# Two layers over a graph on one core: where b_w's row, a weight in squares and the order of the last products stand

## Chip, core and metric

The kernel runs on one core of a Trainium2 chip. The metric is the device time of one execution in microseconds; less is better. A program counts its engines as PE (TensorE, matrix products; PEld is its loading of weights), DVE (VectorE), ACT (ScalarE), POOL (GpSimd) and SP (SyncE, which here only issues transfers). A core has 16 DMA engines, which all queues share.

## What is computed

x is 4096 x 512, adj is a 4096 x 4096 matrix of zeros and ones (int32, 1 in 128 set).

```python
# layer 0
keep   = (adj > 0) & (cumsum(adj > 0, axis=1) <= 64)
cnt    = keep.sum(axis=1)
xj     = leaky_relu((keep @ x / max(cnt, 1)) @ W_nb.T + b_nb)
xi     = leaky_relu(x @ W_line.T + b_line)
x1     = layernorm(x + xi + where(cnt > 0, xj, 0))
# layer 1
Wh     = x1 @ W + b_w
e      = leaky_relu_0.2((Wh @ a1 + b1)[:, None] + (Wh @ a2 + b2)[None, :])
e      = where(adj > 0, e, -9e15)
out    = layernorm(x1 + softmax(e, axis=1) @ Wh)
```

## The kernel before

Rows are worked in 32 blocks of 128. The order of every engine's instructions is that of the program text; nothing reorders them, so what stands ahead in a queue and waits holds up all behind it. Transfers issued from SP and ACT use eight completion semaphores in turn, here called lanes: each transfer first waits until the one eight places before it has landed.

**The maps of layer 0.** `x @ W_nb.T` and `x @ W_line.T` are taken first, block by block (`linear`, L337 to L344). The products need the weights and x turned. Two ways of turning occur. `turn_by_pe` (L279): VectorE copies a chunk of 128 rows with its columns reordered, four products with the identity turn it into PSUM, ACT copies it out. W_nb, W_line (`turn_w`, L328) and block 0 of x go this way. The other is by squares: the transfer puts 32-row bands of the source side by side on 32 partitions each (`load_turned_x`, L265), so that VectorE's transpose of 32 x 32 squares (L294) gives the whole turned tile. Blocks 1 to 31 of x go this way, loaded by POOL.

Behind the weights, SP loads W of layer 1 and the rows a1, a2 and b_w (`load_rows`, L346 to L350). `fold_w` (L352 to L361) multiplies them on VectorE to W @ a1 and W @ a2, and SP writes the result out (L361). The loads of adj (`load_adj`, L160) come next in SP's queue. Each adj chunk of 128 x 2048 goes through ACT (`edge`, L167), the running count on VectorE (`scan`, L179, and L184), and is packed and stored as one byte per entry. VectorE's order within a block of the maps is: turn the block after next, add the bias, add x, then the scans that are due (`codes_until`).

**The sums of layer 0.** For each block, 64 products of 128 x 512 (L509) add up the neighbours' rows, from the turned codes (`make_kt`, L249) and the mapped rows, kept in two parts, y_hi and y_lo. `finish` (L463) does the rest of a block in four parts during the next block's products: scale, add the own row (stored by the maps, loaded by SP, L504), normalise, dot with the folded rows. The scans go on through most of this stage.

**Layer 1's start.** W is loaded (L542), then b_w's row (L546), then x1 as squares (`load_turned`, L561, four transfers for one of 32 steps s), the own row of the last block (L777), and the first codes `nat` (`load_nat`, L608). `turn_x1` (L575) turns the squares of step s; the first three steps' turned tiles lie in `early`, which takes memory of layer 0. For each s, four products give Wh (L809), `finish_wh` (L584) adds b_w's row, and later steps carry the first two blocks' masks and scores and `combine_wh` (L597 to L600), which forms sums of quarters of Wh. At s = 22 and s = 26 `turn` (L685) and `combine` (L698 to L701) prepare the first two parts of the weights.

**Layer 1's sums.** Attention times Wh is done for 256 rows at a time (16 groups g), each in four parts k (q = 4g + k), by a scheme with seven products of half-size matrices instead of eight (`consume`, L710 to L728, on Wh's sums in `bt`). The seven results of a group lie in four PSUM banks, two to a bank and the seventh alone, as `where` (L708) says: (1,2), (4,7), (5,6), 3. The order of the products is that of `order` (L719), another one for the last part of all. The last group's results are put together and written out by the lines from L871 on.

```python
    top, low = (rows.tile([P, 2, HC], F32, name="c") for _ in range(2))
    nc.scalar.copy(top[:, 0], p[1])                 # L876
    tt(top[:, 1], top[:, 0], p[6], ALU.add)         # L877
    tt(top[:, 0], top[:, 0], p[2], ALU.add)         # L878
    tt(low[:, 0], top[:, 1], p[7], ALU.add)         # L879
```

Of the kernel before, what the change touches and what calls it, by code (L numbers as in the profile page):

```python
# [9 lines left out]
F32 = mybir.dt.float32  # L10
# [3 lines left out]
I32 = mybir.dt.int32  # L14
# [6 lines left out]
P = 128  # L21
SQ = 32
# [10 lines left out]
def two_layer_adj_gnn(  # L33
# [16 lines left out]
    nc = tc.nc  # L50
# [86 lines left out]
    with ExitStack() as l0:  # L137
# [117 lines left out]
        with ExitStack() as la:  # L255
# [44 lines left out]
            def early(name):  # L300
                dt = I32 if name == "a" else BF16
                t = adj_p.tile([P, CH], dt, name=name).bitcast(F32)
                return t.rearrange("p (c q) -> p c q", q=C)

            raw = {}
            for name in ("nb", "line"):
                t = early("a")
                raw[name] = [t[:, c, :] for c in range(NC)]
            raw["w"] = []
            for k in range(2):  # L310
                t = early("left")
# [6 lines left out]
            def load_w(name, src, queues):  # L318
                for c in range(NC):
                    queues[c % len(queues)].dma_start(raw[name][c], src[ts(c, P), :])  # L320
# [7 lines left out]
            def turn_w(name, idle=0):  # L328

                wt = wp.tile([P, NC, C], F32, name=f"wt_{name}")  # L330
                for c in range(NC):
                    if idle:
                        spin(idle)
                    turn_by_pe(wt[:, :, ts(c, P)], raw[name][c])
                w_t[name] = wt

            def linear(lhs_t, name):  # L337
                pl = ps_acc.tile([P, C], F32, name="acc")
# [42 lines left out]
            load_own_x(0, nc.sync)  # L381
            load_w("nb", w_nb, (nc.scalar, nc.sync))
            load_turned_x(1)
            load_w("line", w_line, (nc.sync,))
            nc.sync.dma_start(bias_line, b_line.partition_broadcast(P))
            load_w("w", w, (nc.sync,))
            load_rows(nc.sync)
# [5 lines left out]
            for i in range(NB):  # L393
                if i > 1:
                    load_own_x(i - 1, nc.gpsimd)
                if i > 0:
                    load_turned_x(i + 4)
                    turn_x(i + 2)
                xt = xts.pop(i)
                pys[i] = linear(xt, "nb")  # L400
                if i == 0:
                    turn_w("line")
                pls[i] = linear(xt, "line")
                if i == 0:
                    turn_x(1)
                    turn_x(2)
                    load_turned_x(4)
                nc.scalar.copy(y_hi[:, i, :], pys[i])
                if i > 0:
                    line(i - 1)  # L410
                if i > 1:
                    own(i - 2)
                if i == 0:
                    fold_w()
                if i > 0:
                    codes_until(min(i * AHEAD // (NB - 4), AHEAD))
                if i == NB - 3:

                    spare = adj_p.tile([P, CH], I32, name="a")
                    ktbs[0] = spare[:, : CH // 2].bitcast(BF16).rearrange(  # L420
                        "p (t i) -> p t i", t=NT
                    )
                    nc.sync.dma_start_transpose(ktbs[0], code_d[0])
                if i == NB - 1:
                    spare = adj_p.tile([P, CH], BF16, name="edge")
                    kts[0] = spare.bitcast(F32R).rearrange(
                        "p (t r i) -> p t r i", r=2, i=P
                    )
                    make_kt(0)
                nc.vector.tensor_tensor(  # L430
                    y_lo[:, i, :], pys.pop(i), y_hi[:, i, :].bitcast(F32), ALU.subtract
                )
                if i > 0:
                    bend(i - 1)
                if i == NB - 2:
                    load_late()
# [106 lines left out]
            ws[ts(n, SQ), :, :], w[ts(n, P), :].rearrange("(m b) c -> b m c", b=SQ)  # L543
        )
    bias_w = ep.tile([P, C], F32, name="res", bufs=1)
    nc.sync.dma_start(bias_w, b_w.partition_broadcast(P))  # L546


    bt = big.tile([P, NS // 2, 7, HC], F32, name="bt")
# [6 lines left out]
    def load_turned(s):  # L556

        if s < NS:
            part = x1_d[s // 8].rearrange("(n s a) c -> s a n c", s=8, a=SQ)[s % 8]
            for n in range(NC):  # L560
                nc.sync.dma_start(  # L561
                    x1s[ts(n, SQ), s % 4, :].rearrange("a (j c) -> a j c", c=P),
                    part[:, :, ts(n, P)],
                )
# [37 lines left out]
    def load_nat(b, h):  # L602

        if b < NB:
            nats[b, h] = ep.tile([P, 2, NS * SQ // 2], BF16, name="nat")
            rows = code_d[b].rearrange("(i a) (n x) -> n a i x", a=SQ, n=4)
            for n in range(4):
                nc.sync.dma_start(nats[b, h][ts(n, SQ)], rows[n][:, ts(h, 2), :])  # L608
# [96 lines left out]
        }  # L705


    where = {1: (0, 0), 2: (0, 1), 4: (1, 0), 7: (1, 1), 5: (2, 0), 6: (2, 1), 3: (3, 0)}  # L708

    def consume(q):  # L710
        g, k = divmod(q, NP)
        if k == 0:
            two = [ps_s.tile([P, 2, HC], F32, name="pt")]
            two += [ps_acc.tile([P, 2, HC], F32, name="acc") for _ in range(3)]
            banks[g] = {n: two[i][:, j, :] for n, (i, j) in where.items()}
        part = parts.pop(q)


        order = (1, 2, 4, 7, 5, 6, 3) if q < NP * NT - 1 else (4, 1, 2, 6, 7, 5, 3)  # L719
        for n in order:  # L720
            lhs, rhs = part[n]
            mate = [m for m in order if where[m][0] == where[n][0]]
            for j in range(4):
                nc.tensor.matmul(  # L724
                    banks[g][n], lhs[:, j, :], bt[:, 4 * k + j, rhs, :],
                    start=(k == 0 and j == 0 and n == mate[0]),
                    stop=(k == NP - 1 and j == 3 and n == mate[-1]),
                )  # L728
# [46 lines left out]
    for s in range(4):  # L775
        load_turned(s)
    nc.sync.dma_start(owns[NB - 1], own_d[NB - 1])  # L777
    load_nat(0, 0)
    load_nat(0, 1)
    for s in range(3):  # L780
        turn_x1(s)
        load_turned(s + 4)
    for g in range(4):
        finish(NB - 1, g)

# [19 lines left out]
    for s in range(NS):  # L805
        pws[s] = ps_acc.tile([P, C], F32, name="acc")
        x1t = x1ts.pop(s)
        for m in range(NC):
            nc.tensor.matmul(  # L809
                pws[s], x1t[:, m, :], ws[:, m, :], start=(m == 0), stop=(m == NC - 1)  # L810
            )
        if s > 0:
            finish_wh(s - 1)
        turn_x1(s + 3)
        load_turned(s + 7)
        if FIRST <= s < FIRST + 8:
            b, i = divmod(s - FIRST, NI)
            mask(b, i)
            score(b, i)
        if FIRST + 4 <= s < FIRST + 12:  # L820
            b, i = divmod(s - FIRST - 4, NI)
            if i == 0:
                greatest(b)
                shift(b)
            weigh(b, i)
        if s in (FIRST + 14, FIRST + 18):
            q = (s - FIRST - 14) // 4
            turn(q)
            combine(q)
        elif s >= FIRST + 8:  # L830
            combine_wh()
    finish_wh(NS - 1)
# [98 lines left out]
```

## Time and profile before

| | |
|---|---|
| median of 3 runs | 1612.21 us (1611.77 to 1615.34) |
| the profiled execution's own time | 1611.63 us |
| its span, first to last instruction | 1609.9 us |
| PE busy | 1583.8 us (98%) |
| DVE busy | 1328.1 us (82%) |
| ACT busy | 903.2 us (56%) |
| mean granted PE clock | 0.996 |
| maps of layer 0 | to about 236 us |
| sums of layer 0 | to about 704 us |
| Wh | about 710 to 826 us |
| sums of layer 1 | to about 1600 us |

Busy time is an instruction's time on its engine; products are pipelined, so a busy PE isn't PE at its peak. The granted clock is the share of full speed that PE was allowed. The chain of waits is followed back from the last instruction, at each step to what released it. Rows of a timeline give the start, the duration, the engine (SPq is SP's queue), the line, the operation and the tiles; in brackets stand the idle time before it and what ended it.

### The profile page before, as it was taken

What the parts mean: (1) busy time and instruction counts of PE and PEld (TensorE: products, weight loads), DVE (VectorE), ACT (ScalarE), POOL (GpSimd) and SP (SyncE); (2) the same over time, 40 slices, a digit from 0 to 9 for tenths busy, and PEclk for the clock granted to TensorE, in tenths of its full rate; (3) what the DMA queues carried; (4) which work ended last, traced back from release to release, by engine and by line L of the source; (5) the groups of instructions that cost most, each with busy time, mean ns of one, the idle gap of its engine ahead of it and who ended that gap; (6) DMA issues with size and microseconds to landing.
All of it is one profiled execution on the core that took longest, in us unless ns stands there. A gap on an engine that the chain in (4) does not pass through costs nothing.

```text
span 1609.9 us, 18503 instructions
## 1 busy us (share of the span) xinstructions
PE 1583.8 (98%) x6456; PEld 1221.9 (76%) x6456; DVE 1328.1 (82%) x2186; ACT 903.2 (56%) x1054; POOL 258.1 (16%) x396
## 2 busy tenths in 40 slices
PE   9999999999999999989999999999999999999997
PEld 5444448888888787854468888888888888888886
DVE  4999987999999999845798788888788888788863
ACT  2655556677676766413437655567655567655520
POOL 4455532222122222101000000000000000000000
PEclk9999999999999999999999999999999999999999
DMA  8887868767776676335211111111111111111100
GB/s 199 286 264 232 262 211 239 216 202 212 220 208 198 209 213 193 100 103 118 79 40 27 53 40 53 44 29 46 53 41 53 43 30 47 53 40 53 40 7 33
DMA packets 168365, 192.74 MB, mean 120 GB/s; under 512 B 101408, under 2 KB 134464, under 8 KB 160080
## 3 DMA queue, kind: packets, MB, share of 16 engines
q1 hardware_dynamic: 147968, 131.38, 29.6%
q0 software_dynamic: 19728, 59.27, 10.8%
q8 instruction: 50, 0.82, 0.2%
q10 hardware_dynamic: 576, 0.92, 0.2%
q14 instruction: 43, 0.35, 0.1%
HBM read 132.65 MB, written 42.08 MB: 109 GB/s over the span
## 4 chain that ended last, share of the span: by engine, by line
PE 69%; DVE 23%; DMA 3%; issue 2%; ACT 1%; POOL 1%; SPq 0%; DVEq 0%; POOLq 0%; ACTq 0%
PE acc L724 34%; PE pt L724 14%; DVE left L179 10%; PE acc L340 9%; PE acc L509 9%; PE acc L809 3%; DVE left L184 2%; DVE junk L487 2%; DVE own L475 1%; DVE st L117 1%; DVE t L471 1%; DMA a<-in_adj_dram 1%; DVE t L468 1%; DVE own L131 1%; DVE c L575 1%
## 5 line engine op out<-in xcount | busy, mean ns | idle before, releaser
L509 PE MATMUL acc<-y_hi,kt 128*128 128x512 f32 x1016 | 396.3, 390 | 2.9 <-ACT kt L249 2.9
L509 PE MATMUL acc<-y_lo,kt 128*128 128x512 f32 x1016 | 395.8, 390 | 0.0
L724 PE MATMUL acc<-bt,s 128*128 128x256 f32 x1536 | 342.1, 379 | 0.0
L724 PEld LDWEIGHTS acc<-bt,s 128*128 128x128 f32 x1536 | 292.3, 190 | 39.2
L621 ACT ACTIVATE w<-nat,few 128x1024 f32<-128x1024 uint8 x128 | 136.9, 1135 | 277.1 <-DVE a L685 237.0
L126 POOL TENSOR_TENSOR rs<-ve,few 128x1 f32<-128x1 f32 x64 | 76.1, 1190 | 1021.1 <-DVE ve L124 1021.1
L724 PE MATMUL acc<-bt,a 128*128 128x256 f32 x1024 | 231.6, 379 | 0.0
L724 PE MATMUL pt<-bt,a 128*128 128x256 f32 x1024 | 231.5, 379 | 0.0
L509 PEld LDWEIGHTS acc<-y_hi,kt 128*128 128x128 f32 x1016 | 190.7, 188 | 44.5 <-ACT kt L249 5.0
L509 PEld LDWEIGHTS acc<-y_lo,kt 128*128 128x128 f32 x1016 | 190.9, 188 | 39.3
L724 PEld LDWEIGHTS pt<-bt,a 128*128 128x128 f32 x1024 | 194.9, 190 | 26.5 <-issue 0.5
L724 PEld LDWEIGHTS acc<-bt,a 128*128 128x128 f32 x1024 | 194.9, 190 | 26.1
L685 DVE STREAM_TRANSPOSE a<-w 128x1024 f32<-128x1024 f32 x128 | 153.0, 1225 | 56.1 <-ACT w L666 53.2
L249 ACT ACTIVATE kt<-ktb,few 128x1024 fp32r<-128x1024 uint8 x124 | 139.8, 1148 | 84.7 <-PE acc L509 69.0
L167 ACT ACTIVATE edge<-a,few 128x2048 bf16<-128x2048 int32 x64 | 127.9, 1998 | 99.4 <-DVE left L184 78.0
L613 ACT ACTIVATE w<-w,st_n 128x1024 f32<-128x1024 f32 x128 | 149.4, 1234 | 49.8 <-DVE m L624 49.8
L624 DVE CUSTOM_DVE_ANT_0 w<-e_n,w 128x1024 f32<-128x1024 f32 x128 | 149.5, 1221 | 9.1 <-ACT w L621 7.7
L666 ACT ACTIVATE w<-w,nm 128x1024 f32<-128x1024 f32 x128 | 145.4, 1137 | 11.3 <-DVE nm L657 11.3
L179 DVE TENSOR_TENSOR_SCAN left<-few,edge 128x2048 bf16<-128x2048 f32 x32 | 141.3, 4416 | 12.3 <-ACT edge L167 11.2
L179 DVE TENSOR_TENSOR_SCAN left<-few,ends,edge 128x2048 bf16<-128x2048 f32 x32 | 143.2, 4476 | 0.0
L202 ACT CAST code<-left 128x2048 uint8<-128x2048 bf16 x64 | 120.6, 1884 | 7.6 <-DVE left L184 7.6
L340 PE MATMUL acc<-wt_nb,xt 128*128 128x512 f32 x256 | 115.4, 594 | 1.8 <-DVE xt L294 1.0
(135 smaller groups left out, 1528.5 us busy)
## 6 DMA issues: line engine op xcount, KB each, us to landing
a<-in_adj_dram SPq DMA_DIRECT2D x64, 1024.0 KB, 5.7
code_d<-code POOLq DMA_DIRECT2D x64, 256.0 KB, 5.2
nat<-code_d SPq DMA_DIRECT2D x256, 64.0 KB, 2.0
own_d<-xb POOLq DMA_DIRECT2D x32, 256.0 KB, 5.7
w<-x_d SPq DMA_DIRECT2D x128, 64.0 KB, 2.0
c<-in_x_dram POOLq DMA_DIRECT2D x124, 64.0 KB, 5.5
xb<-in_x_dram POOLq DMA_DIRECT2D x31, 256.0 KB, 5.7
own<-own_d SPq DMA_DIRECT2D x31, 256.0 KB, 2.7
```

The costliest lines, as they stand in the source:

```text
L167: nc.scalar.activation(edge_of[s], loaded.pop(s), AF.Sigmoid, bias=steep[:, 0:1], scale=STEEP, accum_out=cnts[:, h, b : b + 1],)
L179: nc.vector.tensor_tensor_scan(left, two.to_broadcast([P, CH]), e, NEIGHBORS + 2.0 if h == 0 else end, ALU.max, ALU.subtract,)
L202: nc.scalar.copy(code.bitcast(U8), seen_of.pop(s))
L249: nc.scalar.activation(kts[s], bytes_.rearrange("p t (i r) -> p t r i", r=2), AF.Sigmoid, bias=steep[:, 1:2], scale=STEEP,)
L340: nc.tensor.matmul(pl, lhs_t[:, k, :], w_t[name][:, k, :], start=(k == 0), stop=(k == NC - 1),)
L509: nc.tensor.matmul(accs[i], kt[:, k // 2, k % 2, :], term[:, j, :], start=(j == 0 and term is y_hi), stop=(j == NB - 1 and term is y_lo),)
L613: nc.scalar.activation(dst, src, AF.Prelu, bias=bias, scale=scale, alpha=0.2)
L621: nc.scalar.activation(w_i, nats[b, i // 2].bitcast(U8)[:, i % 2, :], AF.Relu, bias=far, scale=-FAR)
L624: nc.vector.tensor_tensor_reduce(w_i, e2_n, w_i, 1.0, -3e38, ALU.subtract, ALU.max, m4s[b][:, i : i + 1])
L666: nc.scalar.activation(w_i, w_i, AF.Exp, bias=nms[b][:, i : i + 1], accum_out=z4s[g][:, r, i : i + 1])
L685: nc.vector.transpose(a[:, r].rearrange("p s (i a) -> p i s a", a=SQ), wts[2 * g + r][:, :, ts(k, 8 * SQ)].rearrange("p i (s x) -> p i s x ...
L724: nc.tensor.matmul(banks[g][n], lhs[:, j, :], bt[:, 4 * k + j, rhs, :], start=(k == 0 and j == 0 and n == mate[0]), stop=(k == NP - 1 and ...
```

## The change

Five edits. W_line is loaded as squares of 32 and turned by four VectorE transposes (`turn_line`). The load of b_w's row moves behind the first seven steps of x1's squares, and the first loads of `nat` move into step s = 0. The last group of layer 1 gets its own order of products in all four parts, and the pairs in its banks follow that order: (4,1), (2,6), (7,5), 3. The first two parts' `turn` and `combine` are put at s = 22, 24, 26 and 28, one each.

```diff
-            for name in ("nb", "line"):
-                t = early("a")
-                raw[name] = [t[:, c, :] for c in range(NC)]
+            t = early("a")
+            raw["nb"] = [t[:, c, :] for c in range(NC)]
+
+            line_w = adj_p.tile([P, CH], I32, name="a").bitcast(F32)
+            line_w = line_w.rearrange("p (j c) -> p j c", c=P)
...
+            def turn_line():
+                wt = wp.tile([P, NC, C], F32, name="wt_line")
+                for c in range(NC):
+                    nc.vector.transpose(
+                        wt[:, :, ts(c, P)].rearrange("p m (j a) -> p j m a", a=SQ),
+                        line_w[:, ts(c, NC), :].rearrange("p j (m b) -> p j m b", b=SQ),
+                    )
+                w_t["line"] = wt
...
-            load_w("line", w_line, (nc.sync,))
+            for n in range(NC):
+                nc.sync.dma_start(
+                    line_w[ts(n, SQ)], w_line[:, ts(n, P)].rearrange("(j a) c -> a j c", a=SQ)
+                )
...
-                    turn_w("line")
+                    turn_line()
...
     bias_w = ep.tile([P, C], F32, name="res", bufs=1)
-    nc.sync.dma_start(bias_w, b_w.partition_broadcast(P))
...
-    where = {1: (0, 0), 2: (0, 1), 4: (1, 0), 7: (1, 1), 5: (2, 0), 6: (2, 1), 3: (3, 0)}
+    order = {True: (1, 2, 4, 7, 5, 6, 3), False: (4, 1, 2, 6, 7, 5, 3)}
+    where = {key: {n: divmod(i, 2) for i, n in enumerate(o)} for key, o in order.items()}
...
-            banks[g] = {n: two[i][:, j, :] for n, (i, j) in where.items()}
+            banks[g] = {n: two[i][:, j, :] for n, (i, j) in where[g < NT - 1].items()}
...
-        order = (1, 2, 4, 7, 5, 6, 3) if q < NP * NT - 1 else (4, 1, 2, 6, 7, 5, 3)
-        for n in order:
+        key = g < NT - 1
+        for n in order[key]:
             lhs, rhs = part[n]
-            mate = [m for m in order if where[m][0] == where[n][0]]
+            mate = [m for m in order[key] if where[key][m][0] == where[key][n][0]]
...
-    load_nat(0, 0)
-    load_nat(0, 1)
     for s in range(3):
         turn_x1(s)
         load_turned(s + 4)
+    nc.sync.dma_start(bias_w, b_w.partition_broadcast(P))
...
         load_turned(s + 7)
+        if s == 0:
+            load_nat(0, 0)
+            load_nat(0, 1)
...
-        if s in (FIRST + 14, FIRST + 18):
-            q = (s - FIRST - 14) // 4
-            turn(q)
-            combine(q)
+        if s in range(FIRST + 14, FIRST + 22, 2):
+            q, part = divmod((s - FIRST - 14) // 2, 2)
+            (turn, combine)[part](q)
         elif s >= FIRST + 8:
             combine_wh()
```

## The prediction, made before the changed kernel had run

> **What bounds the kernel now.** I read the page first (PE busy 98% of the span), then the chain of waits, because a busy share doesn't say which wait ends last, and then the timeline and the windows of the three places that the diff touches: the start, the boundary between the layers, the end. From about 714 us on, TensorE (PE) is the bound but for waits of 0.3, 2.2 and 0.7 us near 778, 782 and 818. Between 41 and 84 us and between 292 and 613 us the chain runs over VectorE (DVE), on the scans L179.
>
> The boundary, in SP's timeline (start, duration, what was issued):
>
> ```profile
> 679.99 1.85 SPq L542 DMA_DIRECT2D w<-in_L_gnn_W_dram  x4
> 704.02 0.35 SPq L546 DMA_DIRECT2D res<-in_L_gnn_bW_dram  x1
> 704.41 7.56 SPq L561 DMA_DIRECT2D w<-x_d  x16
> 712.06 0.38 SPq L777 DMA_DIRECT2D w<-own_d  x1
> ```
>
> SP stands still for 22 us in front of L546, the load of b_w's row: its buffer is layer 0's memory, released by the last products of L509. x1's squares (L561) queue behind it though their own buffers are free. The chain of waits in order of time shows what that costs:
>
> ```profile
> 613.22 91.01 PE acc L509 x400
> 704.23 0.14 SPq L546
> ...
> 705.83 2.97 DMA w<-x_d
> ...
> 708.92 0.72 DVE w L575
> ...
> 709.69 10.45 PE acc L809 x17
> ```
>
> PE ends layer 0 at 704.2 and starts layer 1 at 709.69. The windows (last columns: granted PE clock, DMA share, GB/s) show a second price:
>
> ```profile
> 704.00:707.00 3.00, 0.21 (x1) 0.00 (x0) 0.00 (x0) 0.00 (x0) 0.00 (x0) 1.00 0.37 120
> 709.60:712.00 2.40, 2.31 (x3) 1.17 (x4) 1.04 (x3) 0.00 (x0) 0.00 (x0) 0.50 0.53 138
> 712.00:714.00 2.00, 2.00 (x3) 0.67 (x2) 1.74 (x3) 0.00 (x0) 0.00 (x0) 0.50 0.52 162
> 716.00:718.00 2.00, 2.00 (x6) 0.93 (x5) 1.51 (x4) 0.00 (x0) 0.23 (x1) 1.00 0.49 148
> ```
>
> After the gap PE runs at half clock until about 715.5: the first 24 matmuls of L809 take 709.69 to 722.98 = 13.3 us, where 24 at the later pace of 0.429 us take 10.3.
>
> The start, in the same chain:
>
> ```profile
> 9.70 8.40 DMA edge<-in_L_gnn_a_dram
> ...
> 24.07 0.39 SPq L361
> ...
> 24.50 14.51 DMA a<-in_adj_dram
> ...
> 41.16 4.44 DVE left L179
> ```
>
> What sets the pace is not PE. a1's row lands at 18.1, `fold_w` (L356) runs, its result is written (L361), the first adjacency load follows in the same queue, and the first scan starts at 41.16. PE takes xt(5) at 48.4 and xt(6) at 56.5, each made right behind a scan.
>
> The end (start, duration):
>
> ```profile
> 1596.15 3.62 PE L724 MATMUL acc<-bt,s 128*128 128x256 f32 x16
> 1598.14 0.42 DVE L877 TENSOR_TENSOR c<-c,acc 128x256 f32<-128x256 f32 x1 [19.49 <-PE acc L724]
> ...
> 1598.93 0.41 DVE L879 TENSOR_TENSOR c<-c,acc 128x256 f32<-128x256 f32 x1
> ```
>
> L877 reads product 6, complete at about 1594.4, but 6 shares a bank with 5, which ends at 1597.9.
>
> [...] 5.5 us of idleness gave 0.50, while the waits of 1.8 us near 611 and 2.2 us near 782 left it at 1.00. [...] a reader waits for its neighbour in the bank, as L877 does. [...]
>
> **The change, part by part.**
>
> 1. b_w's row behind x1's squares. In the built order the first 16 loads of squares now wait for DMA lanes only, so they issue right after L542, from 681.9 (16 x 0.47 = 7.5 us), and land before 695. The wait for layer 0's last products passes to the load of own row 31 (L777) and to `turn_x1(0)`, whose target lies in layer 0's memory too. Queued behind L777 on SP: squares 4 to 6, then b_w, then squares 7. At 704.05 DVE starts `turn_x1(0)`, 0.71 us; PE starts at 704.05 + 0.71 + 0.06 = 704.8 instead of 709.69: **-4.9 us**. The gap becomes 0.6 us, far below those that left the clock alone: **-3.0 us**. What could be late next: own row 31 is issued at 704.1 and lands 3.6 us later (its delay before), 707.7. DVE's `finish(31)` comes behind three transposes, so L475 starts at about 708.2 (before: 715.73), and `turn_x1(3)` moves from 721.01 to 713.5, done 714.2; PE wants it at 704.8 + 3 x 3.43 = 715.1. Slack 0.9 us. b_w: after 0.4 us of own row and 12 squares x 0.45 from 704.85, issued at about 710.4, landing 3.6 us later at 714.0; `finish_wh(0)` wants it at 714.2. Tight, but PE is five blocks of PSUM away from needing that result.
>
> 2. The 8 loads of nat (1.8 us per 4) move on SP behind squares 7, to about 716 to 720. Squares 8 stand behind them, issued by 722.3, landed by 724.5; their transpose must wait for PE to end s = 5 at 725.4 anyway. ACT wants nat at s = 8, past 732. 0 us.
>
> 3. turn and combine apart (s = 22, 24, 26, 28). DVE has no idle time from 781 to 830, and the burst of 5.0 us at s = 26 (812.7 to 817.7) made `turn_x1(30)` late: PE's weight load at 819.09 shows 0.96 us idle against a usual 0.24. Now only 2.3 us stand there, and the transpose ends some 4 us sooner relative to PE: **-0.7 us**. Two `combine_wh` (1.65 us each) move to q = 0; PE wants their rows at q = 3, some 36 us later. The 0.3 and 2.2 us near 780 come from s = 12 to 19 and stay.
>
> 4. The last group's pairs (4,1), (2,6), (7,5), 3. L877 can start at 1594.7. L879 waits for the bank of 7 and 5, ended 1597.9, so it starts at 1598.14 instead of 1598.93, and all behind it on DVE moves with it: **-0.8 us**. PE does the same number of products in all groups.
>
> 5. The line weight by squares. Off PE: 16 products; off DVE four copies of 0.43; off ACT four copies. On DVE: four transposes of 0.70 = 2.8 us. Each reads all 128 partitions, so all four loads must have landed: before, the fourth had at 12.7 (it frees the lane of L348's third load). Then 12.9 to 15.7, and PE, done with the first map at 14.5, starts the second at 15.8 instead of 17.46. That 1.7 us is **lost**: xt(5) and xt(6) come from DVE behind scans, PE only waits longer for them (about 2 and 1.5 us, short enough for the clock). What counts is when a1 lands. The queues are saturated from 4 to 18 us (DMA share 1.05), so it is what the pieces cost. Rows: 868 packets took 51.8% of 16 engines for 10 us, 95 ns each. Squares of 512 B: at 798 to 816, 24.6% of 16 x 18 us over some 2,410 of them, 29 ns. Per engine 32 x 95 = 3.0 us becomes 128 x 29 = 3.8: **+0.7 us** (estimate), on the chain. Bounds: -0.3[...]; above, from 6 to 12 us, where POOL's squares mix in, the rate fell from 402 to 270 GB/s, which charges some 0.5 MB of squares with about 3.2 us, or +4 us for 1 MB. I take the packet price.
>
> Sum: -4.9 - 3.0 - 0.7 - 0.8 + 0.7 = **-8.7 us**. The profiled execution took 1611.63 us (span 1609.9), 0.6 below the runs' median 1612.21; taken off the median: **1603.5 us**.
>
> **The rivals.**
> - The clock stays halved behind the shorter gap, or the start of layer 1 finds another late input (own row, b_w): 3 us back, 1606.5. Against: 2.2 us gaps didn't do it, and the slack worked out above. 8%.
> - The start costs the upper bound: a1 lands 4 us late[...]: 1606.8 to 1610. For: saturated queues. Against: the packet price. 10%.
> - The change doesn't do what it says: `turn_x1(0)` still waits for something that comes after 704 by a load. Then only parts 3 to 5 count: -0.8, 1611.4. Against: the built order. 3%.
> - Slower: a piece costs by number, not by bytes. L361 writes 1,024 pieces of 4 B and lands after 11.3 us: 64 per engine, 177 ns each. At that price the line squares need 128 x 177 = 22.6 us, 19.6 more; a1 and all behind it are late by that, and 9.4 gained elsewhere leaves 1622. It turns to slower by over 0.2% at about 125 ns a piece. Against: squares of the same 512 B landed in 2.0 us (L561). 3%.
> - The forecast: 76%.
>
> **How the numbers follow.** Predicted is the likeliest case. Low 1601.0: start at -0.3, and another 1.5 for waits near 780 that the earlier start might shorten. High 1607.5 takes in the first rival and most of the second's lower half. 0.2% is 3.2 us, about what a measurement of this kernel tells from no change; faster means below 1609.0. Faster: 0.93; same: 0.04; slower: 0.03.
>
> **What would show it.** After: SP issues L561's successors from 682; PE's gap between the layers under 1 us with the clock at 1.00; first scan at about 41.9; a wait of PE for xt near 47; no idle weight load at s = 30; L879's successor starting 1.5 us before PE's last product ends (1599.6 before). Wrong if the first scan moves by over 2 us, or if a gap of 3 us or more remains between the layers.

## The result, and the profile after

| | before | after |
|---|---|---|
| median, side by side | 1612.56 us (6 runs) | 1606.32 us (6 runs, 1604.27 to 1609.23) |
| ratio | | 0.9961, 95% interval 0.9947 to 0.9975 |
| profiled execution, its span | 1611.63, 1609.9 us | 1609.08, 1607.3 us |
| layer 0's sums begin | 235.2 us | 238.6 us |
| from there to the span's end | 1374.7 us | 1368.7 us |

The gain is 6.3 us, 0.39%, where 8.7 were forecast. The two profiled executions differ by 2.5 us only: the one of after was among the longer of its runs, that of before among the shorter. So the profile is read by stages here.

**The boundary.** SP's timeline of the changed kernel (start, duration, what was issued):

```profile
682.77 1.85 SPq L556 DMA_DIRECT2D w<-in_L_gnn_W_dram  x4
684.66 10.90 SPq L574 DMA_DIRECT2D w<-x_d  x16
708.71 0.34 SPq L791 DMA_DIRECT2D w<-own_d  x1
709.48 5.52 SPq L574 DMA_DIRECT2D w<-x_d  x12
715.05 0.43 SPq L795 DMA_DIRECT2D res<-in_L_gnn_bW_dram  x1
```

The squares of x1 (L574) go out right behind W (L556), and the wait for layer 0's last products now stands in front of the own row (L791). DVE's and PE's timelines at that place:

```profile
708.74 1.90 DVE L588 STREAM_TRANSPOSE w<-w 128x512 f32<-128x512 f32 x3 [8.17 <-issue]
709.51 2.84 PE L822 MATMUL acc<-w 128*128 128x512 f32 x6 [0.64 <-DVE w L588]
```

PE waits 0.64 us in place of 5.5. The windows behind it (third column from the right: granted clock):

```profile
709.60:712.00 2.40, 2.40 (x6) 1.15 (x7) 2.36 (x4) 0.00 (x0) 0.00 (x0) 1.00 0.68 201
712.00:714.00 2.00, 2.00 (x6) 0.85 (x5) 1.78 (x4) 0.00 (x0) 0.00 (x0) 1.00 0.50 133
```

The same windows of before held three products each at 0.50; now six at 1.00.

**The end**, on DVE, and PE's last row:

```profile
1592.91 0.42 DVE L892 TENSOR_TENSOR c<-c,acc 128x256 f32<-128x256 f32 x1 [16.03 <-PE acc L738]
...
1596.31 0.42 DVE L894 TENSOR_TENSOR c<-c,acc 128x256 f32<-128x256 f32 x1 [2.52 <-PE acc L738]
```

```profile
1594.38 3.62 PE L738 MATMUL acc<-bt,s 128*128 128x256 f32 x16
```

L894 (L879 before) starts 1.93 us behind the start of PE's last row; before it was 1598.93 - 1596.15 = 2.78. That is 0.85 us.

**The start** is where the forecast was off. SP's timeline, with the fold's first step on DVE and the first scan:

```profile
2.13 3.30 SPq L396 DMA_DIRECT2D a<-in_L_gnn_W_line_dram  x4
5.48 2.22 SPq L399 DMA_DIRECT2D bias_line<-in_L_gnn_b_line_dram  x1
7.75 2.99 SPq L322 DMA_DIRECT2D left<-in_L_gnn_W_dram  x4
12.08 2.48 SPq L359 DMA_DIRECT2D edge<-in_L_gnn_a_dram  x2
...
26.82 0.39 SPq L372 DMA_DIRECT2D wa_d<-wa  x1
```

```profile
15.64 2.49 DVE L342 STREAM_TRANSPOSE wt_line<-a 128x512 f32<-128x512 f32 x4 [6.09 <-DMA a<-in_L_gnn_W_line_dram]
...
20.95 0.69 DVE L367 SCALAR_TENSOR_TENSOR edge<-left,edge 128x512 f32<-128x512 f32 x1 [1.64 <-DMA edge<-in_L_gnn_a_dram]
...
44.37 4.42 DVE L179 TENSOR_TENSOR_SCAN left<-few,edge 128x2048 bf16<-128x2048 f32 x1 [11.74 <-ACT edge L167]
```

The squares are complete at 15.6 us; before, the fourth row load had landed at 12.7. So a1 is issued at 12.08 instead of 9.70, the fold begins at 20.95 instead of 18.20, and the first scan at 44.37 instead of 41.16. PE's waits (in all, times, longest):

```profile
PE acc L351 <- DVE xt L294: 3.6, 3, 2.2
PE acc L351 <- DVE wt_line L342: 2.9, 1, 2.9
PE acc L822 <- DVE c L588: 2.6, 2, 2.2
PE acc L523 <- ACT kt L249: 2.5, 3, 1.8
```

The second line is new: PE waits 2.9 us for the turned W_line.

**Something that no part of the change explains**: two stretches of half clock, in PE's timeline behind the waits of 1.8 us (shown) and 2.2 us (what decides on them stands under "The clock"):

```profile
616.29 0.50 PE L523 MATMUL acc<-y_hi,kt 128*128 128x512 f32 x1 [1.84 <-ACT kt L249]
...
617.32 0.40 PE L523 MATMUL acc<-y_hi,kt 128*128 128x512 f32 x1
617.55 0.52 PE L523 MATMUL acc<-y_lo,kt 128*128 128x512 f32 x1
617.87 0.63 PE L523 MATMUL acc<-y_hi,kt 128*128 128x512 f32 x1
...
620.43 0.63 PE L523 MATMUL acc<-y_hi,kt 128*128 128x512 f32 x1
620.86 0.50 PE L523 MATMUL acc<-y_lo,kt 128*128 128x512 f32 x1
621.19 0.39 PE L523 MATMUL acc<-y_hi,kt 128*128 128x512 f32 x1
```

From 617.55 to 620.9 the starts lie 0.43 us apart, else 0.23: 3.4 us at half clock, 1.7 us lost. Before had the same two waits without it.

### The profile page after: what moved, and what is told of

Read it like the earlier page. It is cut to its first block, busy times and chain, and to the rows that moved or that the text cites. A ratio compares the mean times of both kernels' runs of the same rounds, so it can differ in the third digit from the quotient of the medians.

```text
span 1607.3 us, 18462 instructions
## 1 busy us (share of the span) xinstructions
PE 1582.5 (98%) x6440; PEld 1219.7 (76%) x6440; DVE 1329.1 (83%) x2186; ACT 901.5 (56%) x1050; POOL 258.8 (16%) x396
## 4 chain that ended last, share of the span: by engine, by line
PE 71%; DVE 21%; DMA 3%; issue 3%; ACT 1%; POOL 1%; SPq 0%; POOLq 0%; DVEq 0%; ACTq 0%
PE acc L738 34%; PE pt L738 14%; DVE left L179 10%; PE acc L351 9%; PE acc L523 8%; PE acc L822 5%; DVE left L184 2%; DVE junk L501 2%; DVE own L489 1%; DVE st L117 1%; DMA a<-in_adj_dram 1%; DVE t L485 1%; DVE t L482 1%; DVE own L131 1%; DMA a<-in_L_gnn_W_line_dram 1%
## 5 line engine op out<-in xcount | busy, mean ns | idle before, releaser
L179 DVE TENSOR_TENSOR_SCAN left<-few,edge 128x2048 bf16<-128x2048 f32 x32 | 141.3, 4417 | 12.8 <-ACT edge L167 11.7
L679 ACT ACTIVATE w<-w,nm 128x1024 f32<-128x1024 f32 x128 | 145.4, 1136 | 11.3 <-DVE nm L670 11.3
```

The lines of the kernel that those rows point to most:

```text
L179: nc.vector.tensor_tensor_scan(left, two.to_broadcast([P, CH]), e, NEIGHBORS + 2.0 if h == 0 else end, ALU.max, ALU.subtract,)
L679: nc.scalar.activation(w_i, w_i, AF.Exp, bias=nms[b][:, i : i + 1], accum_out=z4s[g][:, r, i : i + 1])
```

## The experiments

Twelve kernels beside the changed one, all against before. The last five columns are from each one's profile: first scan, start of PE's second map (W_line), begin of layer 0's sums, time from there to the span's end, and the number of half-clock stretches behind the waits near 612 and 777 us. Four profiles have one more stretch, ahead of the sums: e2 and e11 at 19.4 and 18.0 us, behind the wait for W_line, and e3a and e3b at 51.4 and 50.2 us, behind a wait for xt.

| kernel | median us (runs) | ratio, 95% interval | scan | 2nd map | sums | to the end | half |
|---|---|---|---|---|---|---|---|
| before | | 1 | 41.2 | 17.5 | 235.2 | 1374.7 | 0 |
| after | 1606.32 (6) | 0.9961, 0.9947 to 0.9975 | 44.4 | 18.2 | 238.6 | 1368.7 | 2 |
| e1_line_rows | 1604.80 (5) | 0.9945, 0.9932 to 0.9959 | 42.1 | 16.1 | 236.1 | 1369.0 | 2 |
| e2_line_only | 1615.88 (21) | 1.0009, 1.0003 to 1.0016 | 44.4 | 18.1 | 239.5 | 1374.1 | 0 |
| e3a_long_32 | 1604.96 (1) | | 43.7 | 17.1 | 237.7 | 1365.5 | 0 |
| e3b_short_128 | 1604.81 (1) | | 43.2 | 14.7 | 237.5 | 1365.5 | 0 |
| e4_boundary_only | 1606.07 (5) | 0.9951, 0.9937 to 0.9964 | 42.7 | 16.1 | 236.8 | 1368.7 | 1 |
| e5_split_order | 1612.48 (21) | 0.9989, 0.9982 to 0.9995 | 42.6 | 16.4 | 236.7 | 1374.6 | 1 |
| e6_rows_first | 1606.36 (5) | 0.9954, 0.9941 to 0.9966 | 43.1 | 16.1 | 237.1 | 1367.5 | 1 |
| e7_fill | 1605.26 (5) | 0.9945, 0.9933 to 0.9958 | 43.3 | 16.3 | 237.4 | 1365.8 | 0 |
| e8_squares_wa_late | 1603.78 (5) | 0.9936, 0.9924 to 0.9949 | 35.5 | 17.5 | 234.1 | 1368.7 | 2 |
| e9_rows_wa_late | 1599.77 (4) | 0.9918, 0.9904 to 0.9931 | 34.5 | 16.4 | 232.4 | 1369.0 | 2 |
| e10_wa_late_fill | 1602.86 (5) | 0.9928, 0.9914 to 0.9941 | 35.9 | 17.8 | 235.4 | 1365.7 | 0 |
| e11_squares_fill | 1603.90 (5) | 0.9936, 0.9922 to 0.9949 | 37.2 | 17.5 | 236.7 | 1365.4 | 0 |

Before's median beside e1 and e2 was 1614.02 us, beside e4 to e7 1614.43, beside e8 to e10 1614.36, beside e11 1614.25.

The column "to the end" is the cleanest reading here. Every kernel that holds parts 1 to 4 has 1365.4 to 1365.8 us without a half-clock stretch, 1367.5 with one, 1368.7 to 1369.0 with two: each costs 1.7 us. Rid of them, after (1365.3) lies 9.4 us below before (1374.7). The four terms of the prediction that fall in this part add up to just that: 4.9 + 3.0 + 0.7 + 0.8 = 9.4.

### The parts by themselves

**e1_line_rows**: the changed kernel, with W_line loaded and turned as before.

```diff
-            for n in range(NC):
-                nc.sync.dma_start(
-                    line_w[ts(n, SQ)], w_line[:, ts(n, P)].rearrange("(j a) c -> a j c", a=SQ)
-                )
+            load_w("line", w_line, (nc.sync,))
...
-                    turn_line()
+                    turn_w("line")
```

> The changed kernel with W_line as before (rows, turned by products): edits 1 to 4 alone. Theory A (the squares of W_line cost the start 3.3 us, all of it on the chain): the first scan starts at 41.2 us as before instead of 44.4, and the time is 3.3 us below the changed kernel, about 1603.0, 9.5 below before. Theory B (the start costs nothing in the end, and the missing 2.5 us are waits or half clock elsewhere): first scan at 41.2 too, but the time stays at 1606 to 1607.

**e2_line_only**: before, with that edit of the change alone (the reverse of the diff above, with `turn_line`).

> The kernel before with edit 5 alone (W_line as squares). Theory A: first scan at 44.4, time 3.3 us above before, about 1615.9, or 1 to 2 more if the longer waits of PE for xt halve its clock. Theory B: first scan at 44.4, time within 1 us of before, since PE's 1.7 us of earlier start or later slack takes it up.

Measured: without the squares 0.9945 instead of 0.9961, 2.6 us better, though these two intervals overlap; the squares alone make before slower by 0.09%, 1.5 us, between theory A's 3.3 and theory B's less than 1, and that interval excludes 1. So part 5 is a loss, and its size is known to about 1 us only. How much of it the first scan carries: it starts at 44.4 us in both kernels with squares in this order, and at 41.2, 42.1, 42.7 and 42.6 (mean 42.2) in the four by rows whose start is otherwise unchanged. That is 2.2 us; the sums begin 2.9 later in the mean (239.1 against 236.2). In e2's timeline of PE something more is to be seen:

```profile
11.14 3.70 PE L351 MATMUL acc<-wt_nb,xt 128*128 128x512 f32 x8 [0.67 <-ACT wt_nb L150]
18.14 5.40 PE L351 MATMUL acc<-wt_line,xt 128*128 128x512 f32 x8 [3.30 <-DVE wt_line L342]
```

Eight products take 5.40 us behind the wait for W_line, and 3.70 ahead of it: half clock followed this wait of 3.3 us as well.

**e4_boundary_only**: before, with parts 1 and 2.

```diff
-    nc.sync.dma_start(bias_w, b_w.partition_broadcast(P))
...
-    load_nat(0, 0)
-    load_nat(0, 1)
     for s in range(3):
         turn_x1(s)
         load_turned(s + 4)
+    nc.sync.dma_start(bias_w, b_w.partition_broadcast(P))
...
+        if s == 0:
+            load_nat(0, 0)
+            load_nat(0, 1)
```

> The kernel before with parts 1 and 2 alone (b_w's row and the first nat loads behind x1's squares). Theory A, the prediction's: the gap between the layers shrinks from 5.5 to 0.6 us (-4.9) and the clock stays at 1.00 behind it (-3.0), together -7.9 us, ratio to before 0.9951. Rival B: the clock's 3.0 us come back elsewhere as half-clock stretches behind the 1.8- and 2.2-us waits, so that about -4.5 to -6 us is left, ratio 0.9963 to 0.9972. In the profile: first product of layer 1 within 1 us of layer 0's last under both; under A no other half-clock stretch than before, under B one or two behind those waits.

Measured: 0.9951, 7.9 us of 1614.43 (interval 5.8 to 10.2), as under theory A, and the windows by stage show it:

```profile
700.00:720.00 20.00, 19.36 (x62) 11.28 (x61) 10.16 (x24) 0.23 (x1) 2.88 (x4) 1.00 0.37 91
```

In before this window had 14.53 us of PE and a clock of 0.83. Its profile has one stretch of half clock near 612, which B named; but the ratio has A's number and the interval only just touches B's, so that most of the 3.0 us did not come back elsewhere.

**e5_split_order**: before, with parts 3 and 4.

```diff
-        if s in (FIRST + 14, FIRST + 18):
-            q = (s - FIRST - 14) // 4
-            turn(q)
-            combine(q)
+        if s in range(FIRST + 14, FIRST + 22, 2):
+            q, part = divmod((s - FIRST - 14) // 2, 2)
+            (turn, combine)[part](q)
...
-    where = {1: (0, 0), 2: (0, 1), 4: (1, 0), 7: (1, 1), 5: (2, 0), 6: (2, 1), 3: (3, 0)}
+    order = {True: (1, 2, 4, 7, 5, 6, 3), False: (4, 1, 2, 6, 7, 5, 3)}
+    where = {key: {n: divmod(i, 2) for i, n in enumerate(o)} for key, o in order.items()}
...
```

> The kernel before with parts 3 and 4 alone (turn and combine apart, the last group's pairs). Theory A, from the trace of the changed kernel: -0.4 us behind the 2.2-us wait and -0.85 us at the tail, together -1.2 us, ratio 0.9992. Prediction: -0.7 and -0.8, -1.5 us, 0.9991. Rival: the two combine_wh put off to the sums' start cost there what the split gained, so that only the tail's -0.8 us is left, ratio 0.9995. The boundary's gap of 5.5 us and its half clock must be there as before.

Measured: 0.9989 (0.9982 to 0.9995), 1.8 us; by "to the end", 1374.6 less one stretch of 1.7 against 1374.7, also 1.8. DVE reads the bank of 7 and 5 at 1600.26, 1.93 us behind PE's last row at 1598.33, as in after. The late weight load with 0.96 us of idle time at 819 is gone. The rival is out by the sum, though the interval takes in its 0.9995 at its edge. The three parts together, 7.9 + 1.8 - 1.5 = 8.2 us, agree with the 6.3 of the whole (its interval: 4.0 to 8.5), but only near that interval's upper end.

### Why the squares cost more

**e3a_long_32** and **e3b_short_128** take apart the two things that changed about W_line's loads: rows are pieces of 2 KB into 128 partitions, squares pieces of 512 B into 32. e3a writes long pieces into 32 partitions, e3b short ones into 128.

```diff
+            line_b = line_w.rearrange("p (m k) c -> p m (k c)", k=NC)
...
-                    line_w[ts(n, SQ)], w_line[:, ts(n, P)].rearrange("(j a) c -> a j c", a=SQ)
+                    line_b[ts(n, SQ)], w_line[ts(n, P), :].rearrange("(m b) c -> b m c", b=SQ)    # e3a
+                    line_w[:, ts(n, NC), :], w_line[:, ts(n, P)].rearrange("(k p) c -> p k c", p=P)    # e3b
```

In both the map's weight comes to lie in another order; the work is the same.

> The changed kernel, with W_line still loaded by four transfers into 32 partitions each, but as 2 KB pieces (512 of them, not 2048); W_line's turned values are then in a wrong order, so the first layer's second map is another one; the work is the same. Theory P (the piece of 512 B is what costs): the first scan returns to 41.2 to 41.7 us. Theory Q (writing one transfer into 32 partitions only is what costs): it stays at 44.4.

> The changed kernel, with W_line loaded by four transfers of 512 B pieces (2048 in all, as in the change), but each over all 128 partitions; W_line's values are in a wrong order, the work is the same. Theory P (piece size): the first scan stays at 44 to 44.5 us. Theory Q (32 partitions): it returns to 41.2 to 41.7.

The fold's first step on DVE, first of e3a and then of e3b:

```profile
19.98 0.69 DVE L367 SCALAR_TENSOR_TENSOR edge<-left,edge 128x512 f32<-128x512 f32 x1 [1.70 <-DMA edge<-in_L_gnn_a_dram]
```

```profile
19.38 0.69 DVE L367 SCALAR_TENSOR_TENSOR edge<-left,edge 128x512 f32<-128x512 f32 x1 [3.59 <-DMA edge<-in_L_gnn_a_dram]
```

By rows it begins at 18.20, 18.34, 18.67 and 18.73 (before, e1, e4, e5; mean 18.5), by squares at 20.95 and 20.89. So of 2.4 us about 1.5 come with the 32 partitions alone, and 0.9 with the short pieces alone. Neither is the whole cause; added up they make it. These are single profiles, and rows alone scatter by 0.5 us. By what the target of 32 partitions costs more was not shown.

### What stands between a1 and the first scan

**e6_rows_first**: e1, with a1, a2 and b_w's row loaded ahead of W.

```diff
             nc.sync.dma_start(bias_line, b_line.partition_broadcast(P))
+            load_rows(nc.sync)
             load_w("w", w, (nc.sync,))
-            load_rows(nc.sync)
```

> Parts 1 to 4 with W_line by rows, and the rows a1, a2 and b_w loaded ahead of layer 1's W. Theory A: a1's landing is what the first scan waits for, and W is wanted later; fold_w then begins with W's first quarter, at about 14.5, its result is written at about 20 instead of 24, and the first scan starts at about 38 (42.1 in the kernel with W_line by rows alone); PE's waits for xt near 50 and 58 vanish and the time falls by 1.5 to 3 us against that kernel (1604.8), so about 1602 to 1603, ratio to before 0.993. Rival B: the queues are full, so that what a1 gains W loses; the first scan stays within 1 us of 42 and the ratio stays at 0.9945. Rival C: the first scan comes earlier, but the time stays, since PE's own late start (its first map) sets the pace.

Rival B holds. a1 was issued at 6.1 us, but now the fold waits for W:

```profile
17.92 0.69 DVE L356 SCALAR_TENSOR_TENSOR edge<-left,edge 128x512 f32<-128x512 f32 x1 [2.19 <-DMA left<-in_L_gnn_W_dram]
```

It begins 0.4 us earlier than in e1, and the scan starts at 43.1, no earlier at all. What lies between is shown by windows of before (last columns: DMA share, GB/s):

```profile
20.00:24.00 4.00, 4.00 (x11) 1.71 (x9) 3.83 (x12) 0.00 (x0) 1.68 (x4) 1.00 0.47 135
24.00:36.00 12.00, 12.00 (x29) 5.32 (x28) 5.84 (x14) 3.08 (x4) 4.41 (x8) 1.00 0.66 31
36.00:40.00 4.00, 4.00 (x11) 1.83 (x10) 0.00 (x0) 0.97 (x1) 0.00 (x0) 1.00 1.02 379
```

From 24 to 36 us the queues are busy for two thirds and move 31 GB/s. In that stretch wa_d is under way, the folded rows' write in 1,024 pieces of 4 B, 11.3 us from issue to landing; the 1 MB adjacency load behind it gets its rate at 36 us only. The prediction had the 11.3 us, but not what they do to the load. So:

**e8_squares_wa_late** (the changed kernel) and **e9_rows_wa_late** (e1), with that write put off to block 8 of the maps; it is read at block 30.

```diff
                 nc.vector.tensor_tensor(ca, ca, b12, ALU.add)
-                nc.sync.dma_start(wa_d.rearrange("k (c p) -> p k c", p=P), wa)
...
+                if i == 8:
+                    nc.sync.dma_start(wa_d.rearrange("k (c p) -> p k c", p=P), wa)
```

> The changed kernel with one line moved: the write of the folded rows (wa_d) goes out at block 8 of the maps instead of ahead of the first adjacency load. Theory A: the squares of W_line cost time only through the chain a1, fold_w, wa_d's 1,024 pieces, first adjacency load, first scan. With the load freed from it the first scan starts at about 28 to 31 us (44.4 in the changed kernel), bound by the fold's release of its buffers, the later waits of PE for xt vanish, and the kernel is 3 to 4 us faster than the changed one: ratio to before about 0.9935. What stays is PE's own later second map (18.2 against 16.1 to 17.5 us). Rival B: 1 MB of adjacency loads right behind the weights slows the squares of x, so that PE waits for xt from those instead, and the ratio stays near 0.996.

> The same move of wa_d's write in the kernel with W_line by rows. Theory A: the first scan at about 28 us, PE's two waits for xt (3.1 us) vanish; 2 to 3 us faster than with the write in its old place (ratio 0.9945), so about 0.993; and the squares' kernel with the same move is only 1 to 2 us slower than this one, which is PE's own later start. If the squares cost the same 2.6 us here as without the move, they do not act through the first scan. Rival B: no gain, 0.9945, as with the rows loaded first.

SP's timeline and DVE's first scan in e9:

```profile
15.61 0.33 SPq L350 DMA_DIRECT2D b<-in_L_gnn_b_dram  x1
16.94 19.87 SPq L160 DMA_DIRECT2D a<-in_adj_dram  x4
```

```profile
34.51 4.43 DVE L179 TENSOR_TENSOR_SCAN left<-few,edge 128x2048 bf16<-128x2048 f32 x1 [3.76 <-ACT edge L167]
```

The load goes out at 16.94 instead of 24.6, while the fold still runs, and the scan starts 7.6 us earlier than in e1. Expected were 14. The load itself lands 13.4 us earlier: at 26.52, 9.6 us behind its issue, where in e1 it landed at 39.96, 15.3 us behind its issue at 24.64. So 7.7 us come from the earlier issue and 5.7 from the faster transfer. But in e1 `edge` started at once, at 39.98, and in e9 ACT comes to it only at 32.38, 5.9 us behind the landing, since instructions that wait for DVE and PE stand ahead of it:

```profile
30.48 0.58 ACT L407 CAST y_hi<-acc 128x512 fp32r<-128x512 f32 x1 [1.46 <-PE acc L340]
31.08 1.28 ACT L167 ACT_TABLE_LOAD   x1
32.38 2.00 ACT L167 ACTIVATE edge<-a,few 128x2048 bf16<-128x2048 int32 x1
```

The slow stretch has moved along with the write. In e9 it goes out at 61.75 and lands 18.3 us later, and between 68 and 76 us the queues are full and move little:

```profile
68.00:72.00 4.00, 4.00 (x11) 1.80 (x10) 3.97 (x7) 4.00 (x5) 0.56 (x1) 1.00 0.98 46
72.00:76.00 4.00, 4.00 (x11) 1.81 (x10) 3.93 (x3) 0.37 (x1) 0.00 (x0) 1.00 0.95 93
```

PE waits for nothing there. PE's waits for xt are gone in e9 and 0.2 us in e8. Both gain: e9 5.0 us on e1's median (4.4 by the ratios), e8 4.0 by the ratios on after. e9 is the fastest kernel of the study, 0.9918, 13.2 us below before, and better than both kernels of this case.

But the squares still cost 4.0 us between e8 and e9 (2.9 by the ratios, whose intervals overlap), with the first scan no longer what PE waits for. So the idea that they act through the scan alone gets no support. Part of the difference is clock: three of e9's four runs had a mean clock of 0.998, e8's 0.996 and 0.997. The two profiled executions, both at 0.996 and with two half-clock stretches each, differ by 1.4 us, and PE's second map by 1.0 (17.5 against 16.4). Of that in turn the clock at the very start may be the cause: e9 had it full from 4.2 us on, e8 from 9.0. By rows with the late clock the second map starts at 17.5 (before) and 17.9 (e10) too. e11 below was made to settle this point.

### The clock

**e7_fill** (on e6) and **e10_wa_late_fill** (on e9): products that nobody reads, in the two waits.

```diff
+            if s == 103:
+                fill = ps_s.tile([P, C], F32, name="pt")
+                for n in range(7):
+                    nc.tensor.matmul(
+                        fill, y_hi[:, 0, :P], y_hi[:, 0, :], start=(n == 0), stop=(n == 6)
+                    )
             kt = kts.pop(s)
...
+        if s == 20:
+            fill = ps_s.tile([P, C], F32, name="pt")
+            for n in range(2):
+                nc.tensor.matmul(
+                    fill, ws[:, 0, :P], ws[:, 0, :], start=(n == 0), stop=(n == 1)
+                )
         x1t = x1ts.pop(s)
```

> The kernel with the rows first, and products whose result nobody reads put into two waits of PE: seven of 0.23 us ahead of step 103 of layer 0's sums (a wait of 1.8 us near 612), two of 0.86 us ahead of step 20 of Wh (2.2 us near 777). Theory A: those waits now and then halve PE's clock for some 3.4 us, a loss of 1.7 us each time; with the waits filled there is no window under 0.99 of granted clock in 600:640 and 770:800, the mean clock of every run is 0.998 or more, and the median falls by 1 to 2 us against the kernel without the fill, with a narrower spread. Rival B: the half-clock stretches come by themselves, whatever PE does; then they lie elsewhere or at the same places as often, and the time is the same or up to 0.5 us longer.

The windows around the two waits, of after and of e7:

```profile
600.00:640.00 40.00, 38.16 (x161) 31.10 (x160) 38.29 (x48) 27.38 (x23) 8.46 (x8) 0.96 0.65 193
770.00:800.00 30.00, 27.42 (x60) 11.62 (x59) 25.71 (x59) 11.04 (x19) 0.00 (x0) 0.94 0.30 79
```

```profile
600.00:640.00 40.00, 39.76 (x176) 32.53 (x175) 38.06 (x50) 28.03 (x24) 8.46 (x9) 1.00 0.65 197
770.00:800.00 30.00, 29.13 (x68) 12.50 (x67) 27.42 (x62) 8.71 (x16) 0.00 (x0) 1.00 0.33 84
```

Theory A in all points but one: the clock holds, the runs lie within 0.7 us (e6: 3.1), the median falls by 1.1. Three runs had a mean clock of 0.999; two had 0.997 at nearly the same time. Over all profiles: of the 22 waits at these two places without a fill (before, after and nine experiments), 11 were followed by half clock; of the 6 filled ones (e7, e10, e11) none.

What decides can be read from the profiles, and it isn't mere chance. In each profile the changes of the granted clock lie whole multiples of 3.413 us apart. In after they come at 617.66, 621.08, 781.50 and 784.92; the two drops are 163.84 us apart, 48 times 3.413. In before they come at 708.71 and 715.54, twice 3.413 apart. So in these profiles the clock changed on a grid of windows of this length, and where the grid lay differed from one execution to the next. Here are the windows that end with the two drops of after, and then those of before's grid with the same two waits and no drop (second number: length; third: PE busy):

```profile
614.25:617.66 3.41, 1.57 (x7) 1.16 (x7) 3.38 (x2) 3.41 (x4) 0.54 (x1) 1.00 0.68 207
778.09:781.50 3.41, 1.18 (x4) 0.35 (x3) 3.17 (x8) 3.18 (x6) 0.00 (x0) 1.00 0.03 6
609.72:613.14 3.42, 1.67 (x8) 1.05 (x6) 3.42 (x3) 3.42 (x5) 0.54 (x1) 1.00 0.43 138
780.39:783.80 3.41, 1.72 (x5) 0.41 (x3) 2.41 (x7) 3.18 (x8) 0.00 (x0) 1.00 0.13 37
```

PE was busy for 0.46 and 0.35 of the first two, and for 0.49 and 0.50 of the others. Over the 14 profiles, up to the last product, 18 windows at full clock were followed by half clock: PE was busy for 0.477 of them or less. Of the 6,474 that weren't, all but two (0.46 in e3b, 0.47 in e7) had 0.481 or more. In before and after alone the three drops followed 0.00 (705.30 to 708.71, the gap between the layers), 0.46 and 0.35, and the other 924 windows had 0.487 or more. So in these profiles the clock fell to half behind windows of which PE was idle for 0.523 or more. A wait of 1.84 us is 0.54 of a window, just at that edge; one of 2.23 us is 0.65, over it only where it falls mostly into one window. The fill keeps the window busy: 39.76 us of PE between 600 and 640 us in e7, 38.16 in after.

> W_line by rows, wa_d's write late, and the products whose result nobody reads in PE's waits near 612 and 777 us. Theory A: the two gains add up, 1 to 2 us below the kernel without the fill, runs within 1 us of each other, mean clock 0.998 or more; about 1601 to 1602 us, ratio 0.992 to 0.9925. Rival B: with the scans ahead the wait near 612 has moved or gone, so that the seven products there are only a cost of 1.6 us, and the gain is under 0.5 us.

e10's profile shows the same 1.00 in both windows, and 1365.7 us to the end against e9's 1369.0: 3.3 gained, as A has it. The median says otherwise, 1602.86 against 1599.77, runs from 1599.95 to 1604.49. In the profile the loss is at the start: the clock is full from 9.2 us on against 4.2, the first map begins at 11.2 us against 9.8, and the sums at 235.4 against 232.4. So the sum of the gains was not shown; the start's own scatter of some 3 us hides it.

**e11_squares_fill**: e8 with the same fills, and two more.

```diff
-            spin(12)
+            spin(18)
...
+                    spin(10)
                     turn_line()
```

> W_line by squares, wa_d's write late, and products whose result nobody reads in four places: six more in front of PE's first turn of a block (18 instead of 12), ten in the wait for the turned W_line, seven near 612 us, two near 777 us. It takes the luck of the clock out, to see what the squares themselves cost. Theory A: the squares' landing sets PE's second map; it starts at 17.4 to 18.2 us as in the other kernels with squares (17.5 to 18.2), however early the first map starts, against 16.1 to 16.4 by rows with the clock released early; the runs lie within 1.5 us, about 1 to 2 us above the three fastest runs of the rows' kernel with wa_d late (1599.5 to 1599.8): 1600.5 to 1601.5, ratio 0.9915 to 0.992. Rival B: all that stood between the two kernels was the clock; then 1599 to 1600, ratio 0.991. Rival C: the squares cost their 3 to 4 us in another place: 1603 or more.

PE's timeline:

```profile
9.95 3.70 PE L351 MATMUL acc<-wt_nb,xt 128*128 128x512 f32 x8 [0.68 <-ACT wt_nb L150]
13.49 1.25 PE L328 MATMUL acc<-ident 128*128 128x128 f32 x10
17.45 5.40 PE L351 MATMUL acc<-wt_line,xt 128*128 128x512 f32 x8 [2.71 <-DVE wt_line L342]
```

Theory A's mechanism held and its size did not. The clock is full from 4.4 us on and the first map starts early, at 9.95, but the second still starts at 17.45: the squares' landing sets it. But the time is 1603.9, which is rival C's against e9. Against e10, the kernel by rows with the fills in the two waits, it is 1.0 us (1.3 by the ratios), within the noise; so what the squares cost when the write is late stays open between about 1 and 4 us. The ten products took 1.25 us only, 2.71 of wait were left, and half clock followed: 5.40 us for eight products, where the first map's took 3.70. In the four profiles with squares in this form (after, e2, e8, e11) that wait was 2.7 to 3.3 us, and twice half clock followed it, at 1.7 us: PE was busy for 0.37 (e2) and 0.21 (e11) of the window before the drop, and for at least 0.53 of each window in the other two.

## Why the prediction was right, and where not

**Part 1** was right in each step: loads of squares from 684 us on with nothing to hold them, the wait passed on to the own row, a gap of 0.64 us (0.6 predicted), the clock at 1.00 behind it. e4 gives 7.9 us for the 4.9 and 3.0 that were added up; with an interval of 5.8 to 10.2, that it meets them to the tenth is luck. The slack held too: b_w's row kept DVE's `finish_wh(0)` waiting 0.65 us, but not PE. **Part 2** cost nothing that e4 could show.

**Part 3**: the late weight load vanished as foretold, but the 96 products behind the 2.2-us wait, from the first start to the last, take 40.9 us in e5 instead of 41.25: 0.4 us, not 0.7. The 0.72 us of idle time on the weight loads were not all PE's. **Part 4**: 0.85 us for 0.8. Parts 1 to 4 together: 9.4 us for 9.4. So the rivals of a gap that stays, of a clock that stays halved behind it and of an edit without effect are out.

**Part 5 is the term that was mis-sized**: +0.7 us predicted, +1.5 (e2) to +2.6 (after against e1) measured, and 2.2 at the first scan (3.2 in the two profiles of before and after, over the 2 us that the prediction had named as a sign of being wrong). The step that failed is the price of a piece, 29 ns, taken from a place where the queues had room (24.6% of the 16 engines). On SP's queue, in the first 20 us, before's 2,448 packets take 64.9% of 16 engines, 85 ns each; after's 3,361 take 69.8%. If the other 1,313 cost the same as before, the 2,048 squares cost about 55 ns each (a rough estimate from these rows, since the mix of the others isn't the same). By that price an engine's share grows from 32 x 85 = 2.7 to 128 x 55 = 7.0 us, an upper end for the 2.4 seen at the fold. The prediction had the fall from 402 to 270 GB/s before it and named an upper bound of 3 to 4 us; it chose the quiet price. The measured loss lies about halfway between the two; the rival with 177 ns a piece is far off. e3a and e3b add what the packet price hides: 1.5 us come with the target of 32 partitions at unchanged piece size, a cost that the prediction did not name. In after the rate from 8 to 16 us is 203 and 217 GB/s, where before had 261 and 310.

A second step failed with it: PE was to start its second map earlier, at 15.8 us. It started at 18.18, behind the new wait of 2.9 us, because the squares landed at 15.6 and not at 12.7. The prediction held that PE's start there doesn't matter, since PE waits for xt later anyway; e8 and e11, where those waits are gone, suggest that it is then a cost of its own, but the clock's scatter at the start is as large.

**The clock** was the third: "the waits of 1.8 us near 611 and 2.2 us near 782 left it at 1.00" was true of that one profile and taken for a rule. At these two places 11 of 22 unfilled waits were followed by half clock, by where they fell on the grid, and that before's profile had none was luck. On average this should add the same to before and after, so that it moves the median less than the spread; no run tests that. The forecast of 1603.5 lies 2.8 us below the median; 0.8 to 1.9 of that is part 5, and the rest is within the ratio's interval.

## What to carry to other kernels

Look for a load that queues behind another's wait, and ask which transfer in the queue really needs that wait; here a row of 2 KB held up the inputs of a whole layer for 8 us. Take a transfer's price from a place as crowded as the one it goes to (29 ns a piece where SP's queue took 24.6% of the 16 engines; about 55, an estimate, in the first 20 us of after, where it took 69.8%), and before shortening the wait for a transfer, look whether the queues move bytes at all there: while 4 KB in 4-byte pieces were under way, all that the queues moved came to 31 GB/s for some 11 us. A wait of PE of about 2 us cost another 1.7 us in 11 of 22 cases here, where PE was busy for 0.477 or less of one window of 3.413 us; with products that nobody reads in the wait it was none of 6.

## What the runs showed of the hardware

- PE's granted clock changed on a grid of 3.413 us, and it fell to half behind windows in which PE was busy for 0.477 or less (18 of 18 drops in the 14 profiles, against 2 of 6,474 windows without one; in before and after alone 0.00, 0.35 and 0.46, against 0.487 or more in the 924 others). So of the waits of 1.8 and 2.2 us at two places in the middle 11 of 22 were followed by half clock for 3.41 us, and of those of 2.7 to 3.3 us for W_line 2 of 4. In after 0.46 of busy time was little enough, and the first slower product began 1.3 us after PE had resumed (617.55 against 616.29).
- At the very start PE's first turns of a block run at full clock from 5.0 to 5.4 us on in seven profiles (e1, e4 to e7, e9, e11: four products in 0.66 us, first map from 9.4 to 10.0), and at half clock (1.11 us) until about 9 to 10 us in the other seven (first map from 10.8 to 11.7). That is 1.4 us and more of scatter at the start. Here too it went with the grid, and not with the way in which W_line is loaded: e11, by squares, is among the early, before and e10, by rows, among the late. In the seven early ones a window began at 0.7 to 1.5 us, PE was busy for 0.80 of it or more, and the clock was full at its end, at 4.1 to 4.9. In the others one began at 2.2 to 3.6 us, PE was busy for 0.79 of it or less, and the clock was full only behind the next one, at 9.0 to 10.4.
- 1,024 pieces of 4 B on one queue took 11.3 to 13.0 us at the start and 18 to 19 where they were written later (e8 to e11). All that the queues moved meanwhile came to 31 GB/s in before, and to 46 and 93 in the slow stretch of e9. The 64 KB squares of x issued in that stretch of before landed after 14.0 us, those of the first 46 us in the median after 6.2.
